# Each gather of key and value rows waits until the second gather ahead of it has landed

## The chip, the cores and the metric

The kernel runs on one core of one Trainium2 chip. The metric is the time of one execution on the device in microseconds (us). The kernel before takes 3102.27 us, the median of 11 runs that lie between 3096.76 and 3109.56.

## The reference, cut to what matters

A graph of N = 3327 nodes has a row `x` of 256 numbers for each node and an adjacency matrix with about 0.5% ones, so some 16 neighbours for a node. Four layers follow each other. Layer 0 is a dense graph layer: it averages the rows of the neighbours under a softmax, projects, adds the input and normalizes. Layers 1, 2 and 3 are alike, each with weights of its own:

```python
qkv = layer_norm(x, g1, be1) @ w_qkv              # (N, 3, 8 heads, 32)
scores = einsum('nhd,mhd->hnm', q, k) * 32**-0.5
scores = where(adj != 0, scores, -inf)            # only neighbours count
out = einsum('hnm,mhd->nhd', softmax(scores), v)
x = x + out @ w_proj + b_proj
x = x + gelu(layer_norm(x, g2, be2) @ w1 + b1) @ w2 + b2
```

In these layers a node attends to its neighbours alone. The kernel therefore never forms the N x N scores: it fetches, for each node, the key and value rows of its neighbours.

## The kernel before

**Layer 0** (the first 390 us) multiplies by the whole adjacency matrix on TensorE. Beside that it finds the column numbers of each node's neighbours, counts them, and sorts the nodes by their number of neighbours into a permutation `perm`. It also computes the key, value and query rows of layer 1. A table `kv_dr[L]` in DRAM holds for each layer a row of 512 float32 per node: 256 of the key and 256 of the value.

**Layers 1 to 3** work on 26 blocks of 128 nodes in sorted order, one node on each partition. All nodes of a block have at most `CAPS[b]` neighbours (34 in block 0, 9 in block 25). Blocks 23 to 0 are taken in this order, then 24 and 25. For each of the `CAPS[b]` neighbours of a block, one **gather** (line 640) fetches a row of `kv_dr[L]` for each of the 128 nodes: an indirect DMA on the queue of POOL (GpSimd), 128 rows of 2 KB, 256 KB in all. There are 430 gathers in a layer and 1290 in the three. They are grouped in tiles of 3 or 4 (`SG = 4`), 118 tiles in a layer, 354 in all, which share `SLOTS = 12` buffers called `sl`.

The whole of layers 1 to 3 stands under a manual schedule: each engine works in the order in which `layer` issues the operations, and the framework only adds the semaphores. The loop of `layer` walks over blocks and, within a block, over tiles. At each tile, which the code calls a turn:

- gathers are issued until the loop is `AHEAD = 3` tiles ahead of the tile now used, or until all 12 buffers are held;
- `scores` multiplies the tile's keys by the block's queries on DVE (line 651), in place, and sums over each head (line 652). The queries lie in PSUM, in `qp`, to which ACT copies them (line 634);
- at a block's last tile, `exps` makes the softmax (DVE, and the exponential on ACT);
- the block before this one gets its share of `values`: DVE multiplies the values by the weights in place (line 684), PE transposes them and sums them up in PSUM, in `po` (line 687). That frees the tile's buffer. After the block's last tile ACT copies `po` to `oT` (line 693), and only then are the queries of the next block but one copied to `qp`;
- `turn` lets each unfinished `tail` take one step.

A `tail` does the dense rest of the layer for a pair of blocks (`CHUNKS`), in steps spread over the turns: the projection on PE (lines 542 and 546), the sum on DVE (548), mean and variance on DVE (116 to 119), the inverse root `rsig` on POOL (line 120), three turns later the normalizing (DVE 127, ACT 131), transposes on PE with a copy on ACT (141, 143), the wide layer `pu` on PE (567) with GELU on ACT (571, tile `gT`), the narrow one `pd` on PE (576, 580), and the sum on DVE (585). In layers 1 and 2 the next layer's norm follows in the same way, then its key, value and query rows (PE 161 and 166, ACT 163 and 168), of which POOL scatters the key and value rows to `kv_dr[L + 1]` (line 602, an indirect DMA) and SP stores the queries (606). In layer 3 the result is scattered to the output instead (line 589). In layer 1 POOL also fetches each block's node rows (line 496).

So POOL's queue holds, in the order of the loop: the gathers, and between them `rsig` of the tails, the scatters, and the node rows. A layer's gathers read the whole table `kv_dr[L]`, so its first gather comes behind the last scatter of the layer before. Indirect DMAs take turns on eight semaphores, so each one waits for the DMA eight places ahead of it in POOL's queue. Weights come on SP's queue, at the start of each layer.

A general version of the layers, for graphs that don't fit the caps, stands behind a flag and does not run here.

Of the kernel before, what the change touches and what calls it, by code (L numbers as in the profile page):

```python
# [46 lines left out]
SG = 4  # L47
SLOTS = 12
AHEAD = 3
NODES = 5  # L50
FH = FF // P // 2

# [5 lines left out]
def kernel(ctx: ExitStack, tc: tile.TileContext, ins, out: bass.AP):  # L58
    nc = tc.nc
# [50 lines left out]
    def moments(views, name):  # L110

        n = len(views)
        mv = small.tile([P, 4, 2], FP, tag="mv", name=f"mv_{name}")
        for j, v in enumerate(views):
            st = small.tile([P, 6], FP, tag="st", name=f"st_{name}_{j}")
            nc.vector.bn_stats(st, v)
            nc.vector.bn_aggr(mv[:, j, :], st)
        r = small.tile([P, 4], FP, tag="rsig", name=f"rsig_{name}")
        nc.vector.tensor_scalar(r[:, :n], mv[:, :n, 1], EPS, None, ALU.add)  # L119
        nc.gpsimd.tensor_tensor(r[:, :n], r[:, :n], mhalf[:, :n], ALU.pow)  # L120
        return mv, r

    def normed(pool, views, mv, rs, name):

        n = len(views)
        nm = small.tile([P, 4], FP, tag="nmu", name=f"nmu_{name}")
        nc.vector.scalar_tensor_tensor(nm[:, :n], mv[:, :n, 0], -1.0, rs[:, :n], ALU.mult, ALU.mult)  # L127
        xns = []
        for j, v in enumerate(views):
            xn = pool.tile([P, D], FP, tag="xn", name=f"xn_{name}_{j}")  # L130
            nc.scalar.activation(xn, v, AF.Identity, bias=nm[:, j:j + 1], scale=rs[:, j:j + 1])  # L131
            xns.append(xn)
        return xns
# [337 lines left out]
    with ExitStack() as st:  # L471
# [12 lines left out]
        idx = keep.tile([P, NB, LW], U32, name="idx")  # L484
# [8 lines left out]
        def node_rows(b):  # L493

            nodes_[b] = work.tile([P, NODE], FP, tag="node", bufs=NODES, name=f"node_{b}")
            nc.gpsimd.indirect_dma_start(
                out=nodes_[b], out_offset=None, in_=node_dr[:, :],
                in_offset=bass.IndirectOffsetOnAxis(ap=perm[:, b:b + 1], axis=0))

        def node_list(b):  # L500

            t = nodes_[b]
            cd = t[:, 2 * D:2 * D + CAND]
            nr = (CAPS[b] + 7) // 8
            w = 8 * nr

            cg = work.tile([P, CAND], FP, tag="cg", name=f"cg_{b}")
            nc.vector.scalar_tensor_tensor(cg, cd, 0.0, segb.rearrange("p s k -> p (s k)"), ALU.is_gt, ALU.mult)
            nc.vector.tensor_add(cg, cg, cd)
            ls = work.tile([P, LW], FP, tag="ls", name=f"ls_{b}")  # L510
            for k in range(nr):
                nc.vector.max(out=ls[:, 8 * k:8 * k + 8], in_=cg)
                if k < nr - 1:
                    nc.vector.match_replace(out=cg, in_to_replace=ls[:, 8 * k:8 * k + 8], in_values=cg, imm_value=0.0)
            em = work.tile([P, LW], FP, tag="em", name=f"em_{b}")
            own = work.tile([P, 1], FP, tag="own", name=f"own_{b}")
            nc.vector.tensor_scalar(em[:, :w], ls[:, :w], 0.5, None, ALU.is_lt)
            nc.vector.tensor_scalar(own, pf[:, b:b + 1], 1.0, None, ALU.add)
            nc.vector.scalar_tensor_tensor(ls[:, :w], em[:, :w], own, ls[:, :w], ALU.mult, ALU.add)
            nc.vector.tensor_scalar(idx[:, b, :w], ls[:, :w], -1.0, None, ALU.add)  # L520
            nc.vector.tensor_scalar(bias[:, b, :w], em[:, :w], NEG, None, ALU.mult)
            nc.vector.tensor_reduce(found[:, b, 0:1], em[:, :w], AX.X, ALU.add)
            nc.scalar.copy(found[:, b, 1:2], t[:, 2 * D + CAND:])
            nc.scalar.copy(x_sb[:, b, :], t[:, :D])
# [8 lines left out]
        def tail(L, w, wqn, blocks, oT):  # L533
# [15 lines left out]
            mv, rs = moments(views, f"f{tag}")  # L549
            yield AHEAD  # L550
            xns = normed(work, views, mv, rs, f"f{tag}")
# [41 lines left out]
            mv, rs = moments(views, f"h{tag}")  # L593
            yield AHEAD
            xns = normed(work, views, mv, rs, f"h{tag}")
# [20 lines left out]
        class Attend:  # L616
# [19 lines left out]
            def gather(self, g):  # L636
                a, z = self.cuts[g]
                t = slots.tile([P, SG, 2 * D], FP, tag="slot", name=f"sl_{self.tag}_{g}")
                for k in range(a, z):
                    nc.gpsimd.indirect_dma_start(  # L640
                        out=t[:, k - a, :], out_offset=None, in_=kv_dr[self.L][:, :],
                        in_offset=bass.IndirectOffsetOnAxis(ap=idx[:, self.b, k:k + 1], axis=0))
                self.tiles.append(t)

            def scores(self, g):
# [48 lines left out]
                return True  # L694

        place = {b: (m, j) for m, blocks in enumerate(CHUNKS) for j, b in enumerate(blocks)}
        tails = []
        hidden = []

# [9 lines left out]
        def layer(L):  # L709
# [10 lines left out]
            if first:  # L720
                for b in ORDER[:NODES - 2]:
                    node_rows(b)
# [17 lines left out]
            for k, a in enumerate(att):  # L740
# [3 lines left out]
                for g in range(n):  # L744
                    if first and g == 0:
                        if k + NODES - 2 < NB:
                            node_rows(ORDER[k + NODES - 2])
                        for m in ((1, 2) if k == 0 else (k + 2,)):
                            if m < NB:
                                node_list(ORDER[m])  # L750
                    while sent < turns and held < SLOTS and sent - now <= AHEAD:
                        todo[sent][0].gather(todo[sent][1])
# [219 lines left out]
```

## Time and profile before

| | before |
|---|---|
| median of 11 runs | 3102.27 us |
| lowest, highest | 3096.76, 3109.56 us |
| profiled execution, its own time | 3102.41 us |
| its span | 3100.6 us |
| PE matmul busy | 1783.8 us (58%) |
| PE weight load busy (PEld) | 1368.4 us (44%) |
| DVE busy | 1777.8 us (57%) |
| POOL busy | 1442.0 us (47%) |
| ACT busy | 768.8 us (25%) |
| gathers and scatters (queue q0) | 363.51 MB, 40.3% of 16 engines' span |
| all DMA, mean | 146 GB/s |
| granted TensorE clock, mean | 0.739 |

The busy share of an engine is an average over layer 0 and the three attention layers. The idle time of an engine is put down to what released it: an entry such as "DVE sl L651 <- ACT qp L634" is time in which the DVE stood at line 651 until ACT had written `qp`. The view of waits lists these with their sum, their number and the longest one. "issue" is time in which an engine waited for nothing that the profile shows, and "remote" a wait whose releaser the profile does not find on this core's engines. The timeline shows single instructions: start, duration, line, operation, and in brackets the idle time before it with its releaser.

### The profile page before, as it was taken

The page shows a single profiled execution, that of the slowest core. Times are in us where ns is not written, and L with a number is a line of the kernel's source. Part 1 is how long each engine was busy: PE and PEld are TensorE (multiplying, and loading weights), DVE is VectorE, ACT ScalarE, POOL GpSimd, SP SyncE. Part 2 cuts the span into 40 slices and gives each one's busy share as a digit, 9 for nine tenths or more (in the row PEclk, how much of TensorE's full clock was granted, in tenths as well). Part 3 has the DMA queues.
Part 4 walks back from the last instruction along what each step waited for, and adds up shares of the span by engine and source line. Part 5 has one row for each costly group of instructions (what it writes and reads, how often), then busy time and mean ns, then how long its engine had stood idle before and what let it go on. Part 6 is the DMA issues. An engine that isn't in the chain of part 4 may idle for free.

```text
span 3100.6 us, 25607 instructions
## 1 busy us (share of the span) xinstructions
PE 1783.8 (58%) x8349; PEld 1368.4 (44%) x8349; DVE 1777.8 (57%) x3203; ACT 768.8 (25%) x1420; POOL 1442.0 (47%) x1632
## 2 busy tenths in 40 slices
PE   6777415656656556815656665646634555445556
PEld 5555214444534444614445443535423444334445
DVE  4988546665556666326655655555164456546563
ACT  2877201322212122301322221212301212011112
POOL 0112154554555555154555555563355455555561
PEclk9899756777767776856878776777856767666767
DMA  5664264554545455164555555453354345544551
GB/s 189 210 220 163 80 178 128 148 161 129 155 144 151 141 157 152 49 209 121 150 149 147 155 164 154 141 169 102 115 159 142 113 140 157 167 140 142 147 154 29
DMA packets 154568, 451.23 MB, mean 146 GB/s; under 512 B 30575, under 2 KB 57849, under 8 KB 151097
## 3 DMA queue, kind: packets, MB, share of 16 engines
q0 software_dynamic: 111168, 363.51, 40.3%
q1 hardware_dynamic: 38462, 80.03, 7.6%
q10 hardware_dynamic: 4794, 5.94, 0.6%
q8 instruction: 69, 1.13, 0.2%
q14 instruction: 75, 0.61, 0.1%
HBM read 410.48 MB, written 38.88 MB: 145 GB/s over the span
## 4 chain that ended last, share of the span: by engine, by line
PE 31%; another core or an unknown queue 22%; issue 16%; DVE 15%; ACT 7%; DMA 5%; POOL 4%; ACTq 0%; SPq 0%; DVEq 0%; POOLq 0%
PE pd L580 7%; PE pu L567 6%; PE po L687 6%; PE pk L161 5%; DVE sl L651 3%; DVE sl L684 3%; POOL sl L640 2%; PE pp L546 2%; PE pq L166 2%; DMA sl<-kv,idx 2%; DVE sc L652 2%; ACT gT L571 1%; ACT L571 1%; DMA q<-q 1%
## 5 line engine op out<-in xcount | busy, mean ns | idle before, releaser
L640 POOL DMA_INDIRECT sl<-kv,idx x1290 | 1230.0, 953 | 448.2 <-issue 373.0
L687 PE MATMUL po<-ident,sl 128*128 128x128 f32 x2580 | 496.3, 355 | 717.4 <-DVE sl L684 475.0
L687 PEld LDWEIGHTS po<-ident,sl 128*128 128x128 f32 x2580 | 412.8, 185 | 784.8 <-DVE sl L684 513.3
L651 DVE TENSOR_TENSOR sl<-sl,qp 128x1024 f32<-128x1024 f32 (+1 forms) x354 | 396.7, 1121 | 362.4 <-ACT qp L634 250.3
L580 PE MATMUL pd<-w,gT 128*128 128x256 f32 x1248 | 344.0, 434 | 176.1 <-ACT gT L571 137.4
L567 PE MATMUL pu<-fT,w 128*128 128x256 f32 (+1 forms) x1344 | 358.8, 413 | 131.5 <-issue 94.3
L652 DVE TENSOR_REDUCE sc<-sl 128x32 f32<-128x1024 f32 (+1 forms) x354 | 398.3, 1125 | 15.0 <-DVE sl L651 3.1
L684 DVE TENSOR_TENSOR sl<-sl,qp 128x1024 f32<-128x1024 f32 (+1 forms) x354 | 389.1, 1119 | 2.7
L580 PEld LDWEIGHTS pd<-w,gT 128*128 128x128 f32 x1248 | 267.5, 221 | 240.7 <-ACT gT L571 149.4
L567 PEld LDWEIGHTS pu<-fT,w 128*128 128x128 f32 x1344 | 268.8, 217 | 193.4 <-issue 116.4
L571 ACT ACTIVATE gT<-pu,pv 128x256 f32<-128x256 f32 (+1 forms) x336 | 135.4, 457 | 542.2 <-remote 317.2
L548 DVE TENSOR_TENSOR x_sb<-x_sb,pp 128x512 f32<-128x512 f32 (+1 forms) x42 | 27.3, 650 | 390.3 <-PE pp L546 364.6
L161 PE MATMUL pk<-wq,hT 128*128 128x512 f32 x312 | 190.4, 742 | 100.3 <-ACT hT L143 92.3
L585 DVE TENSOR_TENSOR x_sb<-x_sb,pd 128x512 f32<-128x512 f32 (+1 forms) x42 | 27.3, 649 | 380.8 <-PE pd L580 370.3
L120 POOL TENSOR_TENSOR rsig_f<-rsig_f,mhalf 128x2 f32<-128x2 f32 (+1 forms) x42 | 29.1, 694 | 308.3 <-DVE rsig_f L119 291.7
L602 POOL DMA_INDIRECT kv<-kvr,perm x52 | 52.2, 1004 | 246.9 <-ACT kvr L163 193.6
L693 ACT COPY oT<-po 128x256 f32<-128x256 f32 x78 | 29.1, 373 | 503.9 <-remote 286.6
L131 ACT ACTIVATE xn_f<-x_sb,nmu_f,rsig_f 128x256 f32<-128x256 f32 x78 | 43.3, 594 | 403.7 <-DVE nmu_f L127 297.1
L161 PEld LDWEIGHTS pk<-wq,hT 128*128 128x128 f32 x312 | 68.3, 238 | 160.9 <-ACT hT L143 101.4
L423 DVE MAX8 cand<-abf 128x8 f32<-128x256 bf16 x338 | 119.3, 412 | 0.0
L120 POOL TENSOR_TENSOR rsig_h<-rsig_h,mhalf 128x2 f32<-128x2 f32 (+1 forms) x28 | 19.4, 693 | 197.8 <-DVE rsig_h L119 197.8
L546 PE MATMUL pp<-w_proj,oT 128*128 128x256 f32 x312 | 95.8, 458 | 10.3 <-ACT oT L693 9.9
(217 smaller groups left out, 2026.3 us busy)
## 6 DMA issues: line engine op xcount, KB each, us to landing
a<-in_adj_dram SPq DMA_DIRECT2D x25, 1663.5 KB
sl<-kv,idx POOLq DMA_INDIRECT x1290
kv<-kvr SPq DMA_DIRECT2D x26, 256.0 KB
q<-qr SPq DMA_DIRECT2D x52, 128.0 KB
q<-q SPq DMA_DIRECT2D x52, 128.0 KB
w<-in_L_gnn_w_dram SPq DMA_DIRECT2D x6, 1024.0 KB
node<-x SPq DMA_DIRECT2D x26, 128.0 KB
node<-qr SPq DMA_DIRECT2D x26, 128.0 KB
```

The source lines that it names most:

```text
L161: nc.tensor.matmul(pk, hT[:, c, :], wq[:, c, D:], start=(c == 0), stop=(c == 1))
L166: nc.tensor.matmul(pq[:, :D], hT[:, c, :], wq[:, c, :D], start=(c == 0), stop=(c == 1))
L423: nc.vector.max(out=cand[:, 8 * m:8 * m + 8], in_=ab3[:, m, :])
L546: nc.tensor.matmul(pp[:, j, :], oT[:, c, j * P:(j + 1) * P], w["w_proj"][:, c, :], start=False, stop=(c == 1 and j == n - 1))
L567: nc.tensor.matmul(pu[:, a, :n * P], w["w1"][:, c, f * P:(f + 1) * P], fT[:, c, :n * P], start=(c == 0), stop=(c == 1))
L571: nc.scalar.activation(gT[:, f0 + a, :n * P], pu[:, a, :n * P], AF.Gelu_apprx_tanh, bias=pv[:, L - 1, 8 + f:9 + f])
L580: nc.tensor.matmul(pd[:, j, :], gT[:, f, j * P:(j + 1) * P], w["w2"][:, h * FH + f, :], start=False, stop=(h == 1 and f == FH - 1 and j == ...
L640: nc.gpsimd.indirect_dma_start(out=t[:, k - a, :], out_offset=None, in_=kv_dr[self.L][:, :], in_offset=bass.IndirectOffsetOnAxis(ap=idx[:, ...
L651: nc.vector.tensor_mul(kq, kq, self.qp[:, None, :D].to_broadcast([P, n, D]))
L652: nc.vector.tensor_reduce(self.sc[:, a:z, :], kq.rearrange("p s (h d) -> p s h d", h=HEADS), AX.X, ALU.add)
L684: nc.vector.tensor_mul(vv, vv, self.pw[:, a:z, :, None].to_broadcast([P, n, HEADS, HD]))
L687: nc.tensor.matmul(self.po[:, c, :], t[:, k, D + c * P:D + (c + 1) * P], ident, is_transpose=True, start=False, stop=(a + k == self.S - 1 ...
```

## The change

A list `flight` holds the last two gathers. Each new gather is given a dependency on the older of the two, so POOL does not issue it before that gather's 256 KB have landed. At most two gathers are therefore under way at any time. The list lives through all three layers. Only the gathers of line 640 enter it: the scatters and the node rows neither wait in this way nor are waited for. No operation is added or left out, and each engine's order of work is the same.

```diff
@@ constants
 SLOTS = 12
 AHEAD = 3
+FLIGHT = 2
...
@@ Attend.gather
                 for k in range(a, z):
-                    nc.gpsimd.indirect_dma_start(
+                    ins = nc.gpsimd.indirect_dma_start(
                         out=t[:, k - a, :], out_offset=None, in_=kv_dr[self.L][:, :],
-                        in_offset=bass.IndirectOffsetOnAxis(ap=idx[:, self.b, k:k + 1], axis=0))
+                        in_offset=bass.IndirectOffsetOnAxis(ap=idx[:, self.b, k:k + 1], axis=0)).ins
+                    if len(flight) == FLIGHT:
+                        tc.add_manual_dep(ins, flight.pop(0).name,
+                                          mybir.DependencyInfo(mybir.DependencyClass.Sync, mybir.DependencyReason.DATA),
+                                          reason="gathers in flight")
+                    flight.append(ins)
                 self.tiles.append(t)
...
         place = {b: (m, j) for m, blocks in enumerate(CHUNKS) for j, b in enumerate(blocks)}
+        flight = []
         tails = []
```

## Prediction

> **What bounds the kernel now.** I read the page's chain first, then the costliest groups, then the waits of ACT and of POOL, and last the timelines of single stretches. The page, its chain by engine and the costliest group:
>
> ```profile
> PE 31%; another core or an unknown queue 22%; issue 16%; DVE 15%; ACT 7%; DMA 5%; POOL 4%; ACTq 0%; SPq 0%; DVEq 0%; POOLq 0%
> ...
> L640 POOL DMA_INDIRECT sl<-kv,idx x1290 | 1230.0, 953 | 448.2 <-issue 373.0
> ```
>
> No engine is full: the chain runs through all of them, and 22% of it (682 us) is time for which the profile names no engine. POOL issues the 1290 gathers at 0.95 us, with 0.30 us of "issue" behind each, so one gather per 1.25 us when nothing stops it. From the POOL timeline, the first and the last gather of layers 1, 2, 3 start at 393.24 and 1247.75, 1334.17 and 2141.75, 2226.96 and 3027.47: three gather phases of 854.5, 807.6 and 800.5 us, together 2462.6. In each phase POOL spends 430 x 1.25 = 539 us on gathers, 57, 36 and 30 us on other work, and stands waiting for 253, 232 and 235 us. So a gather has 1.99, 1.88 and 1.86 us of the phase, on average. POOL's waits, then ACT's:
>
> ```profile
> POOL sl L640 <- issue: 373.0, 1210, 3.8
> POOL rsig_f L120 <- DVE rsig_f L119: 291.7, 36, 22.4
> POOL rsig_h L120 <- DVE rsig_h L119: 197.8, 27, 14.9
> POOL kv L602 <- ACT kvr L163: 193.6, 27, 10.9
> ```
> ```profile
> ACT gT L571 <- remote: 317.2, 19, 28.7
> ...
> ACT oT L693 <- remote: 286.6, 15, 41.6
> ...
> ACT hT L143 <- remote: 119.7, 10, 15.5
> ```
>
> POOL waits because DVE and ACT are late, and ACT is late for a reason that the profile calls remote. At the start of layer 2 it can be watched; first PE, then all engines:
>
> ```profile
> 1364.30 1.97 PE L687 MATMUL po<-ident,sl 128*128 128x128 f32 x8 [1.40 <-issue]
> ```
> ```profile
> 1388.05 0.95 POOL L640 DMA_INDIRECT sl<-kv,idx  x1 [0.30 <-issue]
> 1393.22 0.37 ACT L693 COPY oT<-po 128x256 f32<-128x256 f32 x1 [38.49 <-remote]
> ...
> 1393.90 1.22 DVE L651 TENSOR_TENSOR sl<-sl,qp 128x1024 f32<-128x1024 f32 x1 [24.88 <-ACT qp L634]
> ```
>
> The transposes that fill po end at 1366.3. The copy at line 693, which needs nothing else, starts at 1393.22: 27 us later, and 5.2 us after the last of an unbroken run of 44 gathers. DVE stands for 24.9 us behind it. Most of ACT's long remote waits end in this way, 3.5 to 5.5 us after a run's last gather. The trace's semaphore times say the same: in layer 0 all 246 signals of PE are recorded within 0.1 us of their instruction; in the first 2.5 us of a run of gathers 49 of 69; from 8 us on, 17 of 189. (Some records are lost in the runs, so the counts are rough; ACT's late starts are not lost records.) I read this as: **a long run of gathers holds back PE's signals.**
>
> **How long a gather takes to land.** One tile's last gather and the multiply that waits for it:
>
> ```profile
> 400.80 0.95 POOL L640 DMA_INDIRECT sl<-kv,idx  x1 [0.30 <-DMA sl<-kv,idx]
> ...
> 404.62 1.22 DVE L651 TENSOR_TENSOR sl<-sl,qp 128x1024 f32<-128x1024 f32 x1 [3.04 <-DMA sl<-kv,idx]
> ```
>
> That is 3.82 us from the start of the issue to the start of the waiter. Of 354 tiles 38 are waited for in this way: median 3.83, shortest 3.51, longest 4.70. Where all sixteen increments of a landing are recorded, the landing itself is 3.43 us after the start for the first gather of a run, 3.55 for the second, 3.7 within a run. The other 316 tiles lie ready: in the median, a tile's last gather starts 12.8 us before its use.
>
> **The change part by part.** Removed: nothing that costs. Each gather already waits for the eighth DMA ahead in POOL's queue, which never binds (8 x 1.25 = 10 us against 3.7). Added: 1288 waits of a gather for the gather two ahead. The order on every engine stays the same; no instruction is added. At 1.25 us apart, the gather two ahead is 2.5 us old, and no landing is that short, so the wait binds in every run. Two gathers then leave per (landing + wake-up). The trace shows no gather that waits for a landing, so I bound it. From below: 3.43 and 0.15 us, the time in which POOL's line 120 starts behind DVE's line 119; 3.58 a pair, 1.79 a gather. From above: 3.83 and 0.28 us, in which POOL's scatter (line 602) starts behind ACT's copy; 4.11, 2.06 a gather. I take the middle of a run's first two landings, 3.49, since a pair meets nearly empty queues, and 0.25: **3.74 a pair, 1.87 a gather**.
>
> Behind the waiting gather stand, on POOL, lines 120 (rsig, for DVE's line 127), 602 (rows for the next layer, wanted only there), 496 (layer 1) and 589. A late rsig costs little: line 127 stands three turns later in DVE's order, behind tiles whose gathers POOL issues before that rsig.
>
> The sum, with gathers as the bound:
> - outside the gather phases nothing changes: 3102.41 (the profiled execution; its span is 3100.6) less 2462.6 = 639.8;
> - gathers: 3 x 430 x 1.87 = 2412.3;
> - POOL's other work in the phases, 123 us: a pair leaves POOL free for 3.74 - 2.50 = 1.24 us, so I let half of it hide: 61;
> - each layer's first 22 gathers lie beside the weight loads (DMA busy 0.90 in 1336 to 1362, against 0.73 in a plain run), and land in 4.2: 22 x 0.25 x 3 = 16;
> - POOL's waits of 720 us nearly go. The three tiles ahead, 11 gathers, now last 20 us, and the longest recorded wait is 22.4. I leave 10 a layer: 30.
>
> Together **3159**, 57 above the profiled execution, which lies 0.14 above the median of 3102.27. This holds only if the late signals of PE shrink, so that chunks which now take longer than 1.87 us a gather come down to it.
>
> The Trainium skill (DMA: Bandwidth & Descriptors, Anatomy of one DMA — SWDGE (gpsimd) path) gives 2.0 us + bytes / 436e3 for such a transfer. For 256 KB that is 2.60, which with 0.95 of issue and 0.28 of wake-up makes 3.83 a pair, and by it the sum would be 3224; the rows put the data part nearer to 2.5 for a gather that follows idle queues. The same page's Rules for kernel authors speak against the change: issue a DMA early and wait for it late, so that the fixed cost overlaps; by that rule the plain run at 1.25 us should stay, and no run here yet shows what the run's length itself costs.
>
> **The rivals.**
> - *The signals stay late and the lag is passed on* (slower). A tile that lands after its recorded use shifts all that follows. I walked through the recorded starts with 3.74 between a gather and the second after it, and shifted everything whenever a tile landed after its use: 66, 99 and 98 us by the ends of the three layers, so 3102 + 263 = 3365. For it: signals are late 30% of the time even early in a run, and one or two gathers are always in flight. Against it: they grow late with the run's length, and a pair leaves about 1 us without gather packets.
> - *Short runs free the signals, and gathers keep up* (faster). With 1.79 a gather: 639.8 + 2309 + 61 = 3010. It decides where a pair takes under 3.65 us: (3102.4 - 639.8 - 107) / 1290 x 2, with the three additions above. For it: the 682 us of chain without a name, and DVE's 250 us behind ACT's qp. Against: even at 1.79 a layer's gathers need 770 us of the 801 to 855 there are, so most of that chain cannot be won.
> - *The change does nothing*: only if landings took under 2.5 us. The shortest whole one is 3.26. 3102.
>
> **How the numbers follow.** Forecast, gather-bound with signals mostly freed, 3110 to 3230: 0.42. Slower rival, 3230 to 3420: 0.22. Faster rival, 2930 to 3095: 0.28. The last 0.08 are between forecast and faster rival, and the change that does nothing: within 0.2%, which is about what a measurement of this kernel can tell from no change. So faster 0.28, same 0.08, slower 0.64. The range leaves out the outer 0.1 on each side: 3000 to 3350; the forecast's own range is 3110 to 3230.
>
> **What would show it.** Gather starts should alternate, 1.25 and 2.5 us apart, 1.87 on average, in all three phases, and POOL's longest waits should be for landings, at line 640, some 0.6 us x 1290. ACT's remote waits should fall from 850 us to under 300 if signals are freed; if they stay, the slower rival is right. DVE's line 651 should wait for gathers far longer than 79 us. A pair at 3.5 or 4.1 us moves the sum by some 150 us down or 240 up. I am also wrong if PE's signals are late for a reason other than gathers: then ACT's waits stay while runs are gone.

## The result and the profile after

The changed kernel takes **3175.84 us** (median of 8 runs, 3173.2 to 3181.92) against 3102.27 (31 runs): 1.0239 of the time before, 95% interval 1.0224 to 1.0253. The forecast was 3159. The profiled execution took 3171.71 us, its span is 3169.7.

The costliest group, and below it POOL's waits (what waited, for what, us in all, times, longest):

```profile
L641 POOL DMA_INDIRECT sl<-kv,idx x1290 | 1228.6, 952 | 1189.1 <-DMA sl<-kv,idx 899.1
```
```profile
POOL sl L641 <- DMA sl<-kv,idx: 899.1, 853, 4.6
...
POOL kv L603 <- ACT kvr L164: 72.4, 12, 8.7
...
POOL rsig_h L121 <- DVE rsig_h L120: 31.5, 6, 11.4
...
POOL rsig_f L121 <- DVE rsig_f L120: 29.5, 5, 11.9
```

POOL hardly waits for DVE and ACT any more. The two rsig waits and the scatter's wait fall from 683 to 133 us. In their place gathers wait 899 us for landings. ACT's waits, and the wait of DVE that grew most, first before the change and then after it:

```profile
ACT oT L699 <- PE po L693: 524.1, 73, 20.7
ACT xn_f L132 <- DVE nmu_f L128: 396.4, 26, 21.8
ACT gT L572 <- PE pu L568: 377.0, 94, 14.3
```
```profile
DVE sl L651 <- DMA sl<-kv,idx: 78.7, 38, 6.8
```
```profile
DVE sl L657 <- DMA sl<-kv,idx: 994.0, 280, 22.2
```

Not one remote wait is left in ACT's list, where some 850 us stood. Of PE's 693 signals in the gather phases 649 are now recorded within 0.1 us of their instruction, against 337 of 690 before. ACT waits for PE itself, PE for DVE, and DVE for the gathers: 994 us against 79. One stretch of POOL's timeline shows the new pace:

```profile
650.17 0.95 POOL L641 DMA_INDIRECT sl<-kv,idx  x1 [0.30 <-issue]
651.42 0.95 POOL L641 DMA_INDIRECT sl<-kv,idx  x1 [0.30 <-issue]
654.19 0.94 POOL L641 DMA_INDIRECT sl<-kv,idx  x1 [1.82 <-DMA sl<-kv,idx]
655.43 0.95 POOL L641 DMA_INDIRECT sl<-kv,idx  x1 [0.30 <-issue]
658.26 0.94 POOL L641 DMA_INDIRECT sl<-kv,idx  x1 [1.88 <-DMA sl<-kv,idx]
659.51 0.95 POOL L641 DMA_INDIRECT sl<-kv,idx  x1 [0.30 <-issue]
662.35 1.03 POOL L641 DMA_INDIRECT sl<-kv,idx  x1 [1.88 <-DMA sl<-kv,idx]
```

Here a pair leaves every 4.0 to 4.1 us. From the first to the last gather, the three phases now last 858.0, 847.1 and 868.2 us, 2573.3 together against 2462.6. What lies outside them fell from 639.8 to 598.4. So 3171.7 - 3102.4 = 69.3, which is 110.7 more in the phases and 41.4 less outside.

**One thing must be known to read the experiments.** They were run on five occasions, each with runs of the kernel before beside it. On two of these it took 3073 and 3094 us, and the gathers without a limit that were traced there show late signals as in its first trace. On the other three it took 2483, 2478 and 2479, and no kernel's trace there has a remote wait of ACT. Each ratio below is within one occasion, and the text says which kind it was. The records number the chips 6, 6, 7, 3 and 9; number 6 showed 2483 first and 3073 the next time, so the number doesn't separate them. One run of the kernel with five tiles of lead (2658.74 us at a granted clock of 0.714, the others at 0.789) stood apart and is not in its figure.

### The profile page after: what moved, and what is told of

Its sections match the earlier page's. It is cut to its first block, busy times and chain, and to the rows that moved or that the text cites. A ratio compares the mean times of both kernels' runs of the same rounds, so it can differ in the third digit from the quotient of the medians.

```text
span 3169.7 us, 25604 instructions
## 1 busy us (share of the span) xinstructions
PE 1807.1 (57%) x8349; PEld 1392.4 (44%) x8349; DVE 1793.8 (57%) x3203; ACT 768.7 (24%) x1420; POOL 1440.5 (45%) x1632
## 5 line engine op out<-in xcount | busy, mean ns | idle before, releaser
L693 PE MATMUL po<-ident,sl 128*128 128x128 f32 x2580 | 518.1, 370 | 1045.0 <-DVE sl L690 1044.5
L693 PEld LDWEIGHTS po<-ident,sl 128*128 128x128 f32 x2580 | 425.2, 192 | 1133.7 <-DVE sl L690 1083.0
L581 PE MATMUL pd<-w,gT 128*128 128x256 f32 x1248 | 355.2, 445 | 66.9 <-ACT gT L572 61.2
L568 PEld LDWEIGHTS pu<-fT,w 128*128 128x128 f32 x1344 | 279.7, 225 | 131.3 <-ACT fT L144 90.0
L581 PEld LDWEIGHTS pd<-w,gT 128*128 128x128 f32 x1248 | 279.4, 231 | 129.0 <-ACT gT L572 65.1
L162 PE MATMUL pk<-wq,hT 128*128 128x512 f32 x312 | 178.3, 700 | 8.1 <-ACT hT L144 8.0
L668 ACT ACTIVATE sc<-sc 128x136 f32<-128x136 f32 (+11 forms) x78 | 24.4, 313 | 302.3 <-DVE sc L667 287.5
L167 PE MATMUL pq<-wq,hT 128*128 128x256 f32 x312 | 84.8, 396 | 8.2 <-ACT kvr L164 8.2
```

The lines of the kernel that those rows point to most:

```text
L162: nc.tensor.matmul(pk, hT[:, c, :], wq[:, c, D:], start=(c == 0), stop=(c == 1))
L568: nc.tensor.matmul(pu[:, a, :n * P], w["w1"][:, c, f * P:(f + 1) * P], fT[:, c, :n * P], start=(c == 0), stop=(c == 1))
L581: nc.tensor.matmul(pd[:, j, :], gT[:, f, j * P:(j + 1) * P], w["w2"][:, h * FH + f, :], start=False, stop=(h == 1 and f == FH - 1 and j == ...
L668: nc.scalar.activation(scs, scs, AF.Exp, scale=SCALE)
L693: nc.tensor.matmul(self.po[:, c, :], t[:, k, D + c * P:D + (c + 1) * P], ident, is_transpose=True, start=False, stop=(a + k == self.S - 1 ...
```

## The experiments

The theory after the result: (F) gathers set the time of the changed kernel, a pair leaving per landing and wake-up, and the limit of two lets PE's signals through. Rivals: something else sets 3176; or late signals still cost the changed kernel some of its time. On why signals are late: (A) a third gather under way holds them back; (B) gathers that follow without a pause do; (C) only a POOL that stands still lets them through.

### One, three and four gathers under way (kernel before: 2483 us)

```diff
-FLIGHT = 2
+FLIGHT = 1        # also 3, 4
```

> One gather under way at a time; the rest is as in the changed kernel. Theory 'gathers set the time': each gather leaves one landing and one wake-up after the one before. In the changed kernel the first gather of a pair, which meets idle queues, lands 3.34 us after its start (median of its trace); with 0.2 to 0.3 of wake-up that is 3.6 a gather. Outside the gather phases the changed kernel has 3171.7 - 2573.3 = 598 us, so 598 + 1290 x 3.6 = 5240 us, 5150 to 5400 with POOL's other work. ACT's remote waits stay at none. Rival 'something else than gathers sets 3176' (late signals in another place, or DVE): the gathers have slack, and the time stays well under 5000.

> Three gathers under way. At the plain pace of 1.25 us and a landing of 3.7 us the kernel before has about three under way by itself, so this limit binds little: three per (3.9 + 0.25) is 1.38 us a gather. Theory A, 'the number under way holds back the signals, and three is too many': ACT's remote waits stay near 850 us and the time near the kernel before, 3050 to 3130. Theory B, 'they are held back only when the DMA queues never run empty, so any limit below the plain pace frees them': remote waits under 200 us, gathers no longer the bound, 2750 to 2950.

> Four gathers under way. Four times 1.25 us is 5.0 us, longer than nearly every landing (longest wait seen 4.7), so the limit should hardly ever bind. All theories: the kernel before within 1%, 3070 to 3130, with ACT's remote waits near 850 us. A time clearly below would say that a few late landings, not the steady state, start the late signals.

Measured: 5458.77 us for one, 2622.67 for three (1.0569, 1.0551 to 1.0586), 2498.73 for four (1.0064, 1.0044 to 1.0084). With one gather under way the phases last 1615.6, 1620.4 and 1631.8 us, 3.77 a gather and not 3.6. The time is 59 us above the forecast's range. So F holds in kind, and its price was too low, which is taken up below. Three and four lie far below every range that was given for them. On the late signals these three say nothing, since here the kernel before had none (its time is 2483). What they do give is the kernel with signals in time. Four under way is nearly the kernel before; its phases last 653.3, 612.7 and 607.9 us, and its ACT and POOL wait like this:

```profile
ACT oT L699 <- PE po L693: 381.8, 65, 21.3
ACT xn_f L132 <- DVE nmu_f L128: 345.2, 23, 20.3
ACT gT L572 <- PE pu L568: 265.3, 105, 12.8
```
```profile
POOL sl L641 <- issue: 328.1, 1035, 5.9
...
POOL rsig_h L121 <- DVE rsig_h L120: 70.0, 16, 11.4
POOL rsig_f L121 <- DVE rsig_f L120: 67.9, 18, 11.5
POOL sl L641 <- DMA sl<-kv,idx: 57.8, 163, 2.4
```

The program is the same but for 163 short waits, and it takes 600 us less than the kernel before does in its first trace. With signals in time the gathers run near their plain pace (pairs 2.52 us apart in the median), and DVE, PE and ACT follow.

### Spacing without waits (kernel before: 2483 us)

The kernel before, with a power on POOL behind each gather, whose result nothing uses:

```diff
+    pace = const.tile([P, 2], FP, name="pace")
+    nc.vector.memset(pace, 1.0)
...
                         in_offset=bass.IndirectOffsetOnAxis(ap=idx[:, self.b, k:k + 1], axis=0))
+                    nc.gpsimd.tensor_tensor(pace, pace, mhalf[:, :2], ALU.pow)
```

> The kernel before, with no limit on gathers, and behind each gather one small power on POOL (0.72 us, as line 120 has it) that writes a tile nobody reads. Gathers then start some 1.9 us apart, without POOL ever waiting for a landing; with landings of 3.4 us about two are under way. Theory A (number under way) and B (queues that never run empty) both say that the signals come in time: remote waits under 200 us, and 598 + 1290 x 1.92 + some 70 for POOL's other work = 3145 us, 3080 to 3230. Theory C, 'only POOL's standing still lets the signals through': they stay late, remote waits over 500 us, and the time is 3300 or more.

Measured: 3289.02 us, 59 above the range.

```profile
1500.92 1.01 POOL L642 DMA_INDIRECT sl<-kv,idx  x1 [0.18 <-issue]
1501.96 0.73 POOL L645 TENSOR_TENSOR pace<-pace,mhalf 128x2 f32<-128x2 f32 x1
1502.87 1.01 POOL L642 DMA_INDIRECT sl<-kv,idx  x1 [0.18 <-issue]
```

Gathers start 1.95 us apart, and the phases come to 2688.9. That is 1290 x 1.95 = 2515.5 and 173 us more, not 70: POOL's other work, 123 us before the change, finds no wait to hide in, as POOL's waits above 0.35 us in the phases come to 38 us in all. POOL never waits for a landing in this kernel, and it is slower still than the changed one: the pace of the gathers, by whatever means, sets the time. It doesn't tell A, B and C apart, as no signal was late on this occasion.

### Both kernels again (kernel before: 3073 us)

No edit.

> The kernel before, unchanged, for its profile beside the runs of the same chip. The last four kernels ran on a chip on which the kernel before takes 2483 us, not 3102. Theory H, 'the late signals belong to the chip, and the 620 us are theirs': where it takes some 2480 us, its trace shows no remote waits of ACT (under 30 us against 850), POOL's waits for rsig and for the scatter fall from 683 to under 250 us, and a gather phase lasts some 620 us; where it takes some 3100 us, the remote waits are back near 850. Rival H2, 'something else differs between the chips (the clock, or how long a gather lands)': remote waits stay, or landings of the first gather of a run differ from 3.43 us by over 0.3.

> The changed kernel, unchanged. If the gathers alone set its time, it does not depend on whether signals are late in the kernel before: 3130 to 3190 us on any chip, a pair of gathers every 3.8 to 3.9 us. Beside a kernel before of 2483 that is a ratio of 1.27. Rival 'late signals still cost the changed kernel some of its time on the first chip': clearly below 3100 here.

Measured: 3078.16 us for the kernel before (1.0021 of itself, 1.0007 to 1.0036) and 3181.22 for the changed one (1.0354, 1.0327 to 1.0381). ACT's remote waits are back (gT 341.7, oT 252.4, hT 114.7), as H says for a time near 3100. Landings of the first gather of a run are only 0.04 us shorter than in the first trace, so H2's landing is out. The granted clock points to no cause either: the kernel before is granted 0.74 here and 0.80 to 0.81 where it takes 2483, but the changed kernel is granted 0.745 in its traces on both kinds of occasion, and the longer kernels beside 2483 get less than 0.8 as well (0.74 spaced, 0.65 with one under way). H's own wording, that it belongs to the chip, is in doubt: the record names the same number as for 2483.

### Three, four and spaced gathers again (kernel before: 2478 us)

No edit.

> Three gathers under way, once more, to have it beside a kernel before that shows late signals (3070 to 3100 us; where the kernel before shows 2480 again, all three kernels of this call repeat the first call within 0.5%). Theory A, 'a third gather under way holds the signals back': near the kernel before, 3050 to 3130, remote waits of ACT over 500 us. Theory B, 'they are held only when gathers follow at the plain pace without a pause, and a limit of three makes pauses': 2620 to 2800, remote waits under 200 us, faster than both kernels by over 8%.

> Four gathers under way, which hardly ever binds: in the first call 163 waits for a landing, 57.8 us in all. Beside late signals, theories A and B say the same: within 1% of the kernel before, remote waits near 850 us. Only if a few pauses suffice to let the signals through does it fall towards 2500.

> The kernel before with a small power behind each gather, starts 1.95 us apart, no wait for a landing. It took 3289 us where no signal was late. Theories A and B: about two under way, queues that run empty, so the signals are in time here too and the time repeats, 3270 to 3310. Theory C, 'POOL must stand still to let signals through': remote waits over 500 us, and 3450 or more, since POOL works without a pause.

Measured: 2607.36 us (1.0523), 2491.02 (1.0059), 3284.91 (1.325): the same times as on the first of the five occasions, within 0.6%. No signal was late here either, so A, B and C stayed open.

### The changed kernel beside in-time signals, and more lead for a limit of three (kernel before: 2479 us)

The changed kernel has no edit; in the other the loop looks five tiles ahead:

```diff
-FLIGHT = 2
+FLIGHT = 3
+LEAD = 5
...
-                    while sent < turns and held < SLOTS and sent - now <= AHEAD:
+                    while sent < turns and held < SLOTS and sent - now <= LEAD:
```

> The changed kernel unchanged, to have it beside whichever kernel before this call finds: 2480 us with no late signals, or some 3080 with them. Theory 'gathers alone set its time': 3165 to 3190 us beside either. Rival 'what is left of late signals (6% in its first trace) still costs it': below 3130 beside a kernel before of 2480.

> Three gathers under way, and gathers issued up to five tiles ahead in place of three (the tails keep their three turns). With three tiles ahead it took 2607 and 2623 us where no signal was late, 5.5% above the kernel before; DVE stood 351 and 375 us at the keys' multiply for a landing. Beside a kernel before of 2480: if the three tiles of lead are what is short, those waits fall by over 100 us and the time comes to 2500 to 2550; if the pace of the gathers (1.4 us with pauses) is the bound, the time stays at 2600 to 2625. Beside a kernel before of some 3080: theory A, 'a third gather under way holds the signals back', gives 3000 to 3130 with remote waits over 500 us; theory B, 'they are held back only by gathers at the plain pace without a pause', gives 2500 to 2700 with remote waits under 200 us.

Measured: **3176.19 us** for the changed kernel (two runs), here 1.28 of the kernel before (1.2758 to 1.2843). The same time to a fraction of a per cent, beside a kernel before of 3102 and of 2479: late signals cost the changed kernel nothing that its time shows, and the last rival of F falls.

With five tiles of lead, 2619.36 us (median of three runs, 2615.59 to 2623.55; 1.0549, 1.0513 to 1.0584): nothing gained. DVE's waits show why:

```profile
DVE sl L658 <- DMA sl<-kv,idx: 211.0, 97, 21.8
...
DVE nmu_f L129 <- POOL rsig_f L122: 96.4, 25, 11.1
DVE nmu_h L129 <- POOL rsig_h L122: 49.3, 16, 8.0
```

The waits for landings did fall, from 375 and 351 us to 211. But rsig now stands on POOL behind the gathers of two more tiles, and DVE waits 146 us for it, against 8 with a lead of three. One wait took the place of the other.

### One limit for each layer (kernel before: 3094 us)

Layer 1 without a limit, layer 2 with four, layer 3 with three, so that one run has all three side by side:

```diff
-FLIGHT = 2
+FLIGHT = {1: 0, 2: 4, 3: 3}
...
-                    if len(flight) == FLIGHT:
-                        tc.add_manual_dep(ins, flight.pop(0).name,
+                    if FLIGHT[self.L]:
+                        tc.add_manual_dep(ins, flight[-FLIGHT[self.L]].name,
```

> Layer 1 without a limit, as in the kernel before; layer 2 with four gathers under way; layer 3 with three. Read layer by layer, by the length of the gather phase and by ACT's remote waits in it. Beside a kernel before of 2480 (theory H: no late signal there): layer 1 shows what the plain kernel does when signals are in time, 635 to 655 us against 854.5 in its first trace, with no remote wait; layers 2 and 3 repeat 613 and 666; in all 2520 to 2560. Beside a kernel before of some 3080: layer 1 repeats 845 to 855 with remote waits near a third of 850; layer 2 is 790 to 810 with remote waits by theories A and B, under 650 if a few pauses suffice; layer 3 is 780 to 810 with remote waits by theory A (a third gather under way holds signals back), 660 to 700 without them by theory B (only gathers without a pause do).

Measured: 2966.54 us, 0.9597 of the kernel before (0.9567 to 0.9628), faster than the kernel before on an occasion with late signals, and than the changed kernel's 3176 to 3181 elsewhere. The windows of layers 2 and 3 of the kernel before, in its first trace, and of the three phases here (stretch, its length in us, busy us and instructions of PE, PEld, DVE, ACT and POOL, clock, DMA share, GB/s):

```profile
1334.17:2141.75 807.58, 460.68 (x1904) 347.81 (x1904) 458.86 (x639) 165.24 (x320) 445.17 (x471) 0.73 0.53 156
2226.96:3027.47 800.51, 402.87 (x1704) 321.50 (x1704) 444.60 (x574) 128.28 (x240) 438.65 (x462) 0.68 0.52 151
```
```profile
391.14:1239.17 848.03, 477.17 (x1904) 358.48 (x1904) 518.97 (x988) 173.31 (x364) 467.13 (x494) 0.71 0.52 150
1325.10:2123.01 797.91, 460.32 (x1904) 347.53 (x1904) 458.77 (x639) 164.96 (x320) 446.45 (x471) 0.74 0.54 158
2208.10:2891.96 683.86, 396.78 (x1713) 314.83 (x1713) 449.33 (x577) 129.33 (x243) 439.62 (x462) 0.73 0.61 177
```

ACT's remote waits in layer 2, then in layer 3:

```profile
ACT gT L572 <- remote: 119.2, 7, 28.7
...
ACT oT L699 <- remote: 57.6, 3, 37.7
ACT hT L144 <- remote: 53.0, 5, 14.7
```
```profile
...
ACT gT L572 <- remote: 40.0, 7, 10.7
...
ACT oT L699 <- remote: 22.1, 4, 10.6
```

Layer 1 repeats the kernel before (848 against 854.5). Layer 2, with four under way, does so too: 797.9 against 807.6 us, 247 us of remote waits against 274. Layer 3, with three, falls from 800.5 to 683.9 us, and its remote waits from 282 to 62. With signals in time the same limit gave 667.3 and 664.6 in layer 3, so 17 to 19 us are left, which I put down to lateness. **A falls**: three under way don't hold the signals back. It is what B said for a limit of three, but for the remainder. The pause that does it is small: pairs of gathers are 2.85 us apart there in the median, 2.52 in layers 1 and 2. But it comes often: at most 5 gathers in layer 3 follow each other at less than 1.4 us, up to 36 in layer 2. C stays open: in these pauses POOL stands still, and the spaced kernel, which has none of them, ran only where no signal was late. The counts of promptly recorded signals did not follow (82 of 184 in this layer, 101 in the kernel before): records are lost, and ACT's waits are the better witness.

If layers 1 and 2 gained what layer 3 did, a limit of three would take 2966.5 - 2 x 117, some 2730 us, on such an occasion. That was not run there; with signals in time a limit of three costs 5%.

## Why the prediction was right, point by point

- **What bounds the kernel**: right for this occasion, and stronger than it was put. The late signals cost some 620 us, the difference between 3102 and 2479, as far as the traces show it. As a rule, "a long run of gathers holds back PE's signals" is too wide: with four under way, beside 2483, runs of up to 40 gathers at 1.25 us held back none. Taking the long runs away took the late signals' cost away, but a long run alone does not make signals late; what else it takes stays open. A trace of the unlimited kernel on an occasion with in-time signals was not taken; the limit of four stands in for it, 0.6% slower.
- **The limit frees the signals**: right. Remote waits went from 850 us to none, though 44 of PE's 693 signals are still not recorded in time (late or lost), and the changed kernel takes the same time beside either kind of kernel before.
- **Gathers become the bound**: right. DVE waits 994 us for landings, POOL 899, which is 0.70 us x 1290 (0.6 was forecast); the spaced kernel, without a wait for a landing, is slower still (3289).
- **3.74 us a pair**: too low. In the 1084 of 1284 pairs with no other POOL work between them, the mean is 3.88, the median 3.77. With every landing recorded, in the trace beside 2479, landings took 3.45 us on average (3.49 was taken), and most gathers start 0.26 us after the landing (0.25 was taken). What failed is that the wake-up is not one number. 930 gathers carry the wait for the landing themselves and start 0.26 us after it in the median. For 308, of which 295 are the first of a tile, the wait for the landing stands in an instruction of its own ahead of the gather, and they start 0.75 us after it. In the first gather of a tile the place is taken by another wait, for PE to free the buffer. Two waits as such cost nothing: 88 gathers that have another wait ahead of them and carry the landing's themselves start at 0.26. This adds 308 / 1288 x 0.49 = 0.12: 3.45 + 0.26 + 0.12 = 3.83. It also nearly accounts for the run with one gather under way: 3.36 + 0.26 + 0.12 = 3.74 against a measured 3.77. In the sum: 645 pairs x 0.14 = 90 us too little.
- **POOL's other work 61, weights 16, waits that are left 30**: pairs with other work between them have a mean of 4.66, 0.78 more, and each such work falls into two overlapping pairs: 200 x 0.78 / 2 = 78 us. This is what 61 and 30 had to cover, 13 less. The weights' 16 us are within the mean of 3.88: a layer's first 22 gathers have 4.2 us a pair in layers 2 and 3, but 3.7 in layer 1.
- **Outside the phases nothing changes**: wrong, by 41 us the other way. The breaks between the phases fell from 86.4 and 85.2 to 74.6 and 74.0 us, and the end from 73.2 to 57.2. In the kernel before, the last gathers lie ready before their use, with some turns still to go. In the changed one the last tile is used as it lands: after the last gather of layer 1, DVE has 49 instructions left to do and not 60. Signals in time explain the smaller part: with four under way, beside 2483, the breaks and the end are still 83.5, 81.3 and 65.1. Late gathers are partly paid back by a shorter tail.
- So 90 - 16 - 13 = 61 more in the phases, 54 by their measured length, less 41 outside: 13 above the forecast, for the profiled execution. That the total came so close is partly luck: 90 us too little in the price of a pair met 70 us too much elsewhere.
- **Small slips in its sums**: the split of POOL's time closes to 849, 807 and 804 us where the phases are 854.5, 807.6 and 800.5; by its own landing of 3.49 the weights' term would be 23 and not 16; and the sum at 3.83 a pair is 3217, not 3224. None moves the forecast out of its range.
- **Gathers alternate 1.25 and 2.5 us apart**: only in places. Their gaps run evenly from 1.26 to 2.69 us (first and last decile), and only the pair is steady.
- **A late rsig costs little**: right with three tiles of lead (DVE waits 8 us for it), no longer with five (146).
- **The rivals**: the slower one assumed that signals stay late; no remote wait did. The faster one needed a pair under 3.65. Its second thought, that gathers could keep up once signals are free, fits another limit, three under way: in the one layer where that was run beside late signals, the phase is 117 us shorter than in the kernel before.

So the change did what it had to: it took away waits worth 620 us, and the pace of 2 us a gather gave back 697 on top of the kernel with signals in time (3176.19 - 2479.32).

## What to carry to other kernels

When waits for an engine last far longer than its own instructions explain, look at what else runs in those stretches, and run the unchanged kernel beside each experiment: here its time alone told whether there was anything to win. A limit on transfers under way costs (landing + wake-up) / limit for each; choose a limit whose price is well below what the rest needs. By the sum above a limit of three costs (3.68 + 0.26 + 0.12) / 3 = 1.35 us a gather, the kernel with four used 1.41 to 1.52 with signals in time, and three was still 5% slower than no limit. More lead doesn't help where other work stands behind the transfers in the same queue.

## What the runs showed of the hardware

- The same program took 2479 us on some occasions and 3073 to 3102 on others, constant within each. In the longer times ACT starts up to 28.5 us behind the PE instruction that it waits for, during runs of gathers at 1.25 us (427.1 to 455.65 in the first trace; its wait of 41.6 us began earlier), and many semaphore records are missing; in the shorter ones none is late, and all 690 of PE's signals in the gather phases of the kernel with four under way are recorded within 0.1 us. PE's ends are modelled in the profile, so a late signal and a matmul that ends late can't be told apart here. What makes an occasion one or the other stays open. So does whether recording the trace has a part in it: records are lost just where signals are late, and no run is marked as taken without a recording.
- With late signals, a limit of four gathers changed nothing (797.9 us) and one of three nearly all (683.9), although 3.7 us of landing at a pace of 1.25 is three under way already. With three the runs are short (5 gathers at most, against 36); whether it is the length of a run or POOL's standing still that counts was not settled.
- A gather that carried the wait for a landing itself started 0.26 us after it; where that wait stood in an instruction of its own ahead of the gather, 0.75.
